# Cross-attention summaries in a decoder layer: one matmul per head on a quarter of TensorE's columns instead of one per group of four heads

## The chip, the cores and the metric

The kernel runs on one core of a Trainium2 chip. The metric is the device time of one execution in microseconds (us). The kernel before took 1000.46 us in the median of three runs (999.9 to 1000.54).

The core has five engines with their own instruction streams: TensorE (PE in the profile; its weight loads are listed apart as PEld), VectorE (DVE), ScalarE (ACT), GpSimd (POOL) and SyncE (SP), which here starts most DMAs. They wait for one another by semaphores. All arrays are fp32.

## What is computed

The reference is a decoder layer over 8 sequences of 112 tokens with 512 features: causal self-attention, cross-attention with linear features, and a mixture of eight experts, each followed by a residual and a layernorm. The change lies in the cross-attention, which has no softmax. Per batch it sums over the 375 context positions once and then applies the sums to the tokens:

```python
x = layernorm(x + attn(x))
q = feature_map((x @ Wq.T) by heads)          # 16 heads of 32; where(x > 0, x + 1, exp(x))
k, v = split(ctx @ Wkv.T);  k = feature_map(k by heads)
kv_summary = einsum('bhsd,bhse->bhde', k, v)  # per head 32 x 32
k_sum = k.sum(axis=-2)                        # per head 32
z = 1.0 / (einsum('bhld,bhd->bhl', q, k_sum)[..., None] + EPS)
attn = einsum('bhld,bhde->bhle', q, kv_summary) * z
x = layernorm(x + (attn * sigmoid(x @ Wg.T + bg)) @ Wo.T)
x = layernorm(x + experts(x))                 # top 2 of 8
```

## The kernel before

Tokens are kept as seven tiles of 128. Weights stream into nine slabs of 1 MB each, which self-attention, cross-attention and experts use in turn. PSUM has four banks for projections (tag `mm`) and four for everything else (`aux`). From the cross-attention on, the order of each engine's instructions is that of the program text.

The cross-attention goes batch by batch (`for b in range(B)`). The 375 positions of a batch are cut into NSC = 3 chunks of SC = 125. `project_pair(n)` makes keys and values of two chunks at once, with a scheme of seven matrix products for eight: `product` issues two matmuls of 512 columns into one of four banks `kvps_..a` to `kvps_..d`, ScalarE and VectorE combine them (`L779` to `L797`), and `mapped` applies the feature map to the keys (`L770` to `L772`). Keys land in `kf` (125 positions x 3 chunks x 512), values in `values`, with an extra column of ones for each group of heads, so that one matmul gives the summary and the key sum. There are two buffers of each; batch b uses buffer b % 2.

`summarize(b)` is the part that changes. It takes the heads in C = 4 groups of four: 128 key features against 128 value columns and the column of ones, summed over the three chunks. Only the four diagonal 32 x 32 blocks of the 128 x 128 result are wanted, so VectorE multiplies by a block-diagonal mask `bdmask`, once for the key sum, spread over the columns (`bdks`, `L820`), and once for the summary (`bdkv`, `L823`). Two groups share a PSUM bank `sumps`, so this comes in two halves.

`attend(b)` multiplies the query features by `bdks` and `bdkv` (`dps` and `nps`, eight matmuls in all of 112 columns, `L833`), and VectorE divides and applies the gate (`L842` to `L845`). `close(b - 1)` then projects one tile of tokens with Wo (`xops`, `L237`), adds, normalizes and routes it: `x2T_ps` (four transposes), `lps` (128 x 8 scores), `cps` (`L540`, `L541`), a long row of short VectorE operations, and later `sTps` (a product with the identity that turns 128 x 8 scores, `L588`) and `dbps`. These chains are advanced by `tick()` between the parts of the loop:

```python
next(work, None)          # first part of project_pair: kvps a and b
tick()
sums = summarize(b)
tick()
if next(work, 0) is None:
    tick()
attend(b, *sums, qf, gate)
```

So in TensorE's order a batch is: two products of the next pair, the summary, two more products (3.4 us in batches 0 to 5), `dps` and `nps`, the rest of the pair. In the last batch nothing is left to project, and the first steps of the experts run in its place.

Of the kernel before, what the change touches and what calls it, by code (L numbers as in the profile page):

```python
# [10 lines left out]
F32 = mybir.dt.float32  # L11
# [8 lines left out]
P = 128  # L20
# [4 lines left out]
C = D // P  # L25
NH, DH = 16, 128
G = 4
SC, NSC = 125, 3
XH = 32
# [16 lines left out]
def decoder_layer(ctx: ExitStack, tc: tile.TileContext, t_in: dict, out: bass.AP):  # L46
    nc = tc.nc
# [12 lines left out]
    def bank(name: str, tag: str = "mm"):  # L60
        return psum.tile([P, 512], F32, tag=tag, name=name)
# [21 lines left out]
    bdmask = const.tile([P, P], F32, name="bdmask")  # L83
# [166 lines left out]
    with tc.tile_pool(name="att", bufs=2) as att:  # L250
# [201 lines left out]
        for h in range(NH + 1):  # L452
            g = h // G
# [231 lines left out]
    with tc.tile_pool(name="cross", bufs=2) as cr:  # L685
# [12 lines left out]
        keys_of = [cr.tile([SC, NSC, 512], F32, name=f"kf{i}", bufs=1) for i in range(2)]  # L698

        values = [  # L700
            cr.tile([SC, NSC, C, P + 1], F32, name=f"values{i}", bufs=1) for i in range(2)
        ]
        for v in values:
            nc.gpsimd.memset(v[:, :, :, P:], 1.0)

        def load_context(b: int):
            cT = cr.tile([P, C, SC * NSC], F32, tag="cT", name=f"cT_{b}")
# [6 lines left out]
        pairs = []  # L714
# [17 lines left out]
        def blocks_of(n: int):  # L732
            one, two = (contexts[b][:, :, sc * SC : (sc + 1) * SC] for b, sc in pairs[n])
            return one[:, low], two[:, low], one[:, high], two[:, high]

        def prepare_pair(n: int):
            if n < len(pairs):
                b11, b12, b21, b22 = blocks_of(n)
                t = room["sums"][n % 2]
                nc.gpsimd.tensor_sub(t[:, 0], b12, b11)  # L740
                nc.gpsimd.tensor_sub(t[:, 1], b22, t[:, 0])
                nc.gpsimd.tensor_sub(t[:, 2], b22, b12)
                nc.gpsimd.tensor_sub(t[:, 3], b21, t[:, 1])

        def project_pair(n: int):

            b11, _, b21, b22 = blocks_of(n)
            t, (e1, e2) = room["sums"][n % 2], room["ends"]
            k1, k2 = (keys_of[b % 2][:, sc, :] for b, sc in pairs[n])
            v1, v2 = (values[b % 2][:, sc, :, :P] for b, sc in pairs[n])  # L750

            def grouped(x):
                return x.rearrange("p (g e) -> p g e", g=C)

            def product(ps, x, w, start: bool):

                for c in range(C // 2):
                    nc.tensor.matmul(
                        ps,
                        x[:, c, :],  # L760
                        w[:, c, :],
                        start=start and c == 0,
                        stop=c == C // 2 - 1,
                        skip_group_check=not start,
                    )

            def mapped(k, name: str):

                tmp = cr.tile([SC, 512], F32, tag="tmp", name=f"{name}_{n}")
                nc.vector.tensor_scalar_min(tmp, k, 0.0)  # L770
                nc.scalar.activation(tmp, tmp, AF.Exp)
                nc.vector.scalar_tensor_tensor(k, k, 0.0, tmp, ALU.max, ALU.add)  # L772


            order = "ab" if n % 2 else "ba"
            got = {i: bank(f"kvps_{n}{i}")[:SC, :] for i in order + "cd"}
            pa, pb, pc, pd = (got[i] for i in "abcd")
            product(pa, b11, wk[:, low], True)
            nc.scalar.copy(e1, pa)  # L779
            product(pb, b21, wk[:, high], True)  # L780
            nc.vector.tensor_add(k1, e1, pb)
            if n != 1:
                prepare_pair(n + 1)
            yield
            product(pa, t[:, 1], wkvs[1], False)
            nc.scalar.copy(e2, pa)
            product(pc, t[:, 0], wkvs[0], True)
            nc.vector.tensor_add(k2, e2, pc)
            mapped(k1, "one")
            yield  # L790
            product(pa, t[:, 2], wkvs[2], False)
            nc.scalar.copy(e1, pa)
            nc.vector.tensor_add(v2, grouped(e1), grouped(pc))
            product(pd, b22, wkvs[3], True)
            nc.vector.tensor_add(k2, k2, pd)
            product(pa, t[:, 3], wv[:, high], False)
            nc.scalar.copy(v1, grouped(pa))  # L797
            mapped(k2, "two")

        def summarize(b: int):  # L800

            kf, vs = keys_of[b % 2], values[b % 2]
            bdkv = cr.tile([P, C, P], F32, tag="bdkv", name=f"bdkv_{b}")
            bdks = cr.tile([P, C, P], F32, tag="bdks", name=f"bdks_{b}")
            mask = bdmask.unsqueeze(1).broadcast_to([P, 2, P])
            for i in range(2):
                ps = bank(f"sumps_{b}_{i}", "aux")
                sums = ps[:, : 2 * (P + 1)].rearrange("p (g e) -> p g e", g=2)
                for j in range(2):
                    g = 2 * i + j  # L810
                    for sc in range(NSC):
                        nc.tensor.matmul(  # L812
                            sums[:, j, :],
                            kf[:, sc, g * P : (g + 1) * P],
                            vs[:, sc, g, :],
                            start=(sc == 0),
                            stop=(sc == NSC - 1),
                        )
                pair = slice(2 * i, 2 * i + 2)
                nc.vector.tensor_mul(  # L820
                    bdks[:, pair, :], mask, sums[:, :, P:].broadcast_to([P, 2, P])
                )
                nc.vector.tensor_mul(bdkv[:, pair, :], mask, sums[:, :, :P])  # L823
            return bdkv, bdks

        def attend(b: int, bdkv, bdks, qf, gate):
# [26 lines left out]
        for n in range(2):  # L853
            for _ in project_pair(n):
                pass
# [8 lines left out]
        for n, w in (("xq", wxq), ("xg", wxg)):  # L864
            for g in range(C):
                for half in range(2):
                    cols = slice(half * HALF, (half + 1) * HALF)
                    ps = bank(f"{n}ps_{g}_{half}")
# [137 lines left out]
        for b in range(B):  # L1006
            if b + 1 < B:

                ns = (3 * b // 2 + 2,) if b % 2 == 0 else (3 * (b + 1) // 2, 3 * (b + 1) // 2 + 1)
                work = itertools.chain.from_iterable(  # L1010
                    itertools.chain(project_pair(n), (None,)) for n in ns
                )
            else:
                work = iter(())
                steps = [start(0, side, "bT")]
                ahead_w.append(fetch_weights(1))
                third = fetch_in_parts(2)
                ahead_w.append(next(third))
            next(work, None)
# [9 lines that stand above are left out]
            if 0 < b < B - 1:  # L1029
                chains.append(close(b - 1))  # L1030
                tick()
            for _ in work:
                tick()
            if b + 3 < B:
                load_context(b + 3)


    with tc.tile_pool(name="moe", bufs=2, reuse_waits="tile") as moe:
# [8 lines left out]
        sums = keep.tile([P, C, T], F32, tag="big", name="sums", bufs=2)  # L1047
        sums = sums.rearrange("p c n -> p (c n)")
# [260 lines left out]
```

## Time and profile before

| | |
|---|---|
| median of three runs | 1000.46 us |
| the profiled execution | 998.96 us |
| its span, first to last instruction | 997.4 us |
| TensorE's granted clock, mean | 0.993 of full speed |
| cross-attention's batches in that span | about 525 to 745 us |
| in 525 to 745: TensorE, VectorE, ScalarE busy | 212.0, 138.0, 60.6 us of 220 |
| summary matmuls (`sumps`), instructions and busy time | 192, 23.4 us |
| idle time of TensorE before `sumps` | 1.8 us, once, for `kf` of batch 1 |
| idle time of VectorE until `sumps` is done | 12.8 us in 16 waits |
| share of the DMA engines busy, 525 to 745 | 0.24; 0.90 in 720 to 760 |

How to read the lines in the prediction: a timeline line gives the start in us from the span's first instruction, the time until the last of the merged instructions ends, the engine, the line of the kernel, the operation, output and inputs, their shapes (weights, then moving operand for a matmul), the count, and in brackets the idle time before and what ended it. Matmuls overlap: one of 129 columns is listed with 0.275 us although the next starts 0.112 us later; the pitch of a row is therefore (time of the row - duration of the last) / (count - 1). A tile query lists each kind of instruction that writes or reads a tile with the shortest, middle and longest duration in ns. A line of the chain of waits gives start, length and what held the end up at that time.

### The profile page before, as it was taken

The numbers are of one execution on the slowest core, as the hardware profiler recorded it, in microseconds if no ns is written. First come the engines' busy times: TensorE is split into PE (matmuls) and PEld (weight loads), VectorE is DVE, ScalarE is ACT, GpSimd is POOL, SyncE is SP. The second block draws the span as 40 slices with busy tenths as digits, with TensorE's granted clock in tenths as the row PEclk, the third lists the DMA queues.
The fourth block names the chain that finished last, engine by engine and source line by source line (L and its number), as shares of the span: only waits on it lengthen the run. The fifth ranks groups of instructions, "written<-read, shape, count | busy, mean of one in ns | idle before, by whom it ended". The sixth has DMA issues, their size and how long they took to land.

```text
span 997.4 us, 9419 instructions
## 1 busy us (share of the span) xinstructions
PE 963.8 (97%) x3271; PEld 505.1 (51%) x3271; DVE 462.5 (46%) x1036; ACT 244.7 (25%) x430; POOL 185.2 (19%) x235
## 2 busy tenths in 40 slices
PE   7998999999999999999999999999899999999994
PEld 3455544566446555654555455555454444444442
DVE  1356511154213542574414566567775533334384
ACT  1132311133103311322222222333124211121132
POOL 3133200033001414020002222211101212111132
PEclk9999999999999999999999999999999999999998
DMA  9990004111010001131001010110489997692333
GB/s 337 367 342 26 1 1 168 43 42 44 0 46 39 1 1 43 43 104 31 1 0 31 9 50 36 53 63 32 151 346 370 328 391 218 202 344 46 95 86 82
DMA packets 33839, 114.99 MB, mean 115 GB/s; under 512 B 3845, under 2 KB 8005, under 8 KB 26240
## 3 DMA queue, kind: packets, MB, share of 16 engines
q1 hardware_dynamic: 26784, 98.28, 26.9%
q0 software_dynamic: 6336, 15.75, 6.6%
q8 instruction: 26, 0.43, 0.2%
q10 hardware_dynamic: 672, 0.36, 0.1%
q14 instruction: 21, 0.17, 0.1%
HBM read 115.83 MB, written 29.01 MB: 145 GB/s over the span
## 4 chain that ended last, share of the span: by engine, by line
PE 86%; DVE 7%; issue 3%; ACT 1%; POOL 1%; DMA 1%; SPq 0%; POOLq 0%; DVEq 0%; ACTq 0%
PE gups L1054 13%; PE ops L237 10%; PE yps L1080 6%; PE vps L327 6%; PE zps L435 3%; PE xqps L870 2%; PE xgps L870 2%; PE sumps L812 2%; PE sps L387 2%; PE xops L237 2%; DVE z L843 1%; PE pps L427 1%; PE aT_ps L975 1%; PE bT_ps L975 1%; DVE p L412 1%
## 5 line engine op out<-in xcount | busy, mean ns | idle before, releaser
L1054 PE MATMUL gups<-slab,bT 128*128 128x512 f32 x336 | 151.5, 593 | 2.0 <-ACT bT L979 2.0
L1054 PEld LDWEIGHTS gups<-slab,bT 128*128 128x128 f32 x336 | 61.9, 190 | 71.4 <-issue 68.4
L237 PE MATMUL ops<-slab,zT 128*128 128x512 f32 x224 | 97.9, 592 | 0.0
L1062 DVE TENSOR_TENSOR gu<-gups,biases 128x512 f32<-128x512 f32 x42 | 29.0, 691 | 114.8 <-PE gups L1054 114.8
L1080 PE MATMUL yps<-slab,aT 128*128 128x512 f32 x168 | 75.9, 595 | 2.3 <-ACT aT L979 2.3
L237 PEld LDWEIGHTS ops<-slab,zT 128*128 128x128 f32 x224 | 42.0, 190 | 50.3 <-issue 49.5
L275 POOL TENSOR_TENSOR ws<-slab 128x256 f32<-128x256 f32 x16 | 11.8, 739 | 282.0 <-PE qk_5c L291 83.0
L327 PE MATMUL vps<-slab,x0T 128*112 128x512 f32 x128 | 58.6, 612 | 1.0 <-DVE x0T L187 0.8
L1094 POOL DMA_INDIRECT total<-y,nums x19 | 30.4, 1602 | 134.6 <-ACT y L1091 61.2
L1080 PEld LDWEIGHTS yps<-slab,aT 128*128 128x128 f32 x168 | 31.2, 190 | 40.6 <-issue 37.1
L244 DVE TENSOR_TENSOR xn<-xn,ops 128x512 f32<-128x512 f32 x28 | 19.2, 685 | 55.3 <-PE ops L237 55.2
L435 PEld LDWEIGHTS zps<-pT,v 112*128 112x128 f32 x256 | 33.5, 192 | 12.3 <-issue 11.2
L327 PEld LDWEIGHTS vps<-slab,x0T 128*112 128x112 f32 x128 | 22.8, 183 | 31.3 <-issue 29.7
L442 DVE COPY zT<-zps 128x448 f32<-128x448 f32 x32 | 20.0, 624 | 39.8 <-PE zps L435 39.8
L411 DVE TENSOR_REDUCE nm<-p 112x4 f32<-112x448 f32 x32 | 19.7, 616 | 30.9 <-POOL p L401 30.9
L435 PE MATMUL zps<-pT,v 112*128 112x112 f32 x256 | 33.4, 273 | 0.0
L1091 ACT COPY y<-yps 128x512 f32<-128x512 f32 x20 | 11.7, 584 | 87.8 <-issue 79.8
L237 PE MATMUL xops<-slab,gate 128*128 128x512 f32 x56 | 27.3, 632 | 3.8 <-DVE gate L845 2.6
L1066 ACT ACTIVATE sg<-gu 128x512 f32<-128x512 f32 x21 | 13.2, 630 | 71.2 <-DVE gu L1064 53.6
L565 POOL DMA_INDIRECT store<-xn,rows x14 | 13.9, 992 | 81.3 <-DVE count L627 52.5
L395 ACT ACTIVATE p<-sps 112x448 f32<-112x448 f32 x32 | 17.4, 544 | 45.6 <-PE sps L387 45.6
L387 PE MATMUL sps<-k,q 128*112 128x112 f32 x256 | 28.0, 262 | 0.0
(799 smaller groups left out, 1649.4 us busy)
## 6 DMA issues: line engine op xcount, KB each, us to landing
slab<-in_wg_dram SPq DMA_DIRECT2D x21, 1024.0 KB
slab<-in_wu_dram SPq DMA_DIRECT2D x21, 1024.0 KB
slab<-in_wd_dram SPq DMA_DIRECT2D x21, 1024.0 KB
store<-slab SPq DMA_DIRECT2D x8, 1806.0 KB
biases<-gubs SPq DMA_DIRECT2D x21, 512.0 KB
cT<-in_ctxT_dram SPq DMA_DIRECT2D x8, 750.0 KB
xblk<-store POOLq DMA_DIRECT2D x21, 258.0 KB, 7.4
slab<-in_wq_dram SPq DMA_DIRECT2D x4, 1024.0 KB
```

The source lines that it names most:

```text
L237: nc.tensor.matmul(ps, aT[:, c, t * P : (t + 1) * P], w[:, c, :], start=(c == 0), stop=(c == C - 1),)
L327: nc.tensor.matmul(ps[:S, :], xT[:, c, b * S : (b + 1) * S], w[:, c, :], start=(c == 0), stop=(c == C - 1),)
L387: nc.tensor.matmul(ps[:S, i * S : (i + 1) * S], qk["q"][:, rows], qk["k"][:, rows], start=True, stop=True,)
L435: nc.tensor.matmul(zps[:, i * S : (i + 1) * S], v[:, half * 4 + i, hl * DH : (hl + 1) * DH], pT[:, i * S : (i + 1) * S], start=True, stop= ...
L442: nc.vector.tensor_copy(zT[:, hl, half * HALF : (half + 1) * HALF], zps[:, :HALF])
L812: nc.tensor.matmul(sums[:, j, :], kf[:, sc, g * P : (g + 1) * P], vs[:, sc, g, :], start=(sc == 0), stop=(sc == NSC - 1),)
L870: nc.tensor.matmul(ps[:, :HALF], w[:, c, g * P : (g + 1) * P], xT[:, c, cols], start=(c == 0), stop=(c == C - 1),)
L975: nc.tensor.transpose(ps[:, c * P : (c + 1) * P], src[:, c * P : (c + 1) * P], ident)
L1054: nc.tensor.matmul(ps, st["bT"][:, c, :], st["w"][k][:, c, :], start=(c == 0), stop=(c == C - 1),)
L1062: nc.vector.tensor_add(a, ps, st["bias"][:, k * I : (k + 1) * I])
L1080: nc.tensor.matmul(ps, st["aT"][:, c, :], st["wd"][:, c, :], start=(c == 0), stop=(c == C - 1 and s < STEPS - 1),)
L1094: put = nc.gpsimd.indirect_dma_start(out=total, out_offset=bass.IndirectOffsetOnAxis(ap=st["num"], axis=0), in_=y, in_offset=None, compute ...
```

## The change

The summary is made head by head. `values` gets a column of ones for each of the NH = 16 heads (XH = 32 columns and one) instead of each group. For each of the four groups and three chunks there are four matmuls, one per head j of the group: 32 key features as weights, 33 moving columns, and the output on PSUM partitions 32j to 32j + 31, which places the head's weights on TensorE's columns 32j to 32j + 31 (a tile of 128 rows x 32 columns). The off-diagonal blocks are not computed. The results of all four groups stand side by side in one PSUM bank, 4 x 33 columns. VectorE then fills `bdks` and `bdkv` with one operation each of 128 x 512 in place of two of 128 x 256, multiplying by the same mask; for `bdkv` the 32 columns of a head are read four times. The rest of the diff adapts the writers of `values` to 16 pieces of 32 columns and the memset of the ones from 4 to 16 columns per chunk.

```diff
         values = [
-            cr.tile([SC, NSC, C, P + 1], F32, name=f"values{i}", bufs=1) for i in range(2)
+            cr.tile([SC, NSC, NH, XH + 1], F32, name=f"values{i}", bufs=1) for i in range(2)
         ]
         for v in values:
-            nc.gpsimd.memset(v[:, :, :, P:], 1.0)
+            nc.gpsimd.memset(v[:, :, :, XH:], 1.0)
...
-            v1, v2 = (values[b % 2][:, sc, :, :P] for b, sc in pairs[n])
+            v1, v2 = (values[b % 2][:, sc, :, :XH] for b, sc in pairs[n])
 
             def grouped(x):
-                return x.rearrange("p (g e) -> p g e", g=C)
+                return x.rearrange("p (h e) -> p h e", h=NH)
...
-            mask = bdmask.unsqueeze(1).broadcast_to([P, 2, P])
-            for i in range(2):
-                ps = bank(f"sumps_{b}_{i}", "aux")
-                sums = ps[:, : 2 * (P + 1)].rearrange("p (g e) -> p g e", g=2)
-                for j in range(2):
-                    g = 2 * i + j
-                    for sc in range(NSC):
+            ps = bank(f"sumps_{b}", "aux")
+            sums = ps[:, : C * (XH + 1)].rearrange("p (g e) -> p g e", g=C)
+            for g in range(C):
+                for sc in range(NSC):
+
+                    for j in range(C):
+                        h = g * C + j
                         nc.tensor.matmul(
-                            sums[:, j, :],
-                            kf[:, sc, g * P : (g + 1) * P],
-                            vs[:, sc, g, :],
+                            sums[j * XH : (j + 1) * XH, g, :],
+                            kf[:, sc, h * XH : (h + 1) * XH],
+                            vs[:, sc, h, :],
                             start=(sc == 0),
                             stop=(sc == NSC - 1),
                         )
-                pair = slice(2 * i, 2 * i + 2)
-                nc.vector.tensor_mul(
-                    bdks[:, pair, :], mask, sums[:, :, P:].broadcast_to([P, 2, P])
-                )
-                nc.vector.tensor_mul(bdkv[:, pair, :], mask, sums[:, :, :P])
+            nc.vector.tensor_mul(
+                bdks,
+                bdmask.unsqueeze(1).broadcast_to([P, C, P]),
+                sums[:, :, XH:].broadcast_to([P, C, P]),
+            )
+            nc.vector.tensor_mul(
+                bdkv.rearrange("p g (j e) -> p g j e", j=C),
+                bdmask.rearrange("p (j e) -> p j e", j=C)
+                .unsqueeze(1)
+                .broadcast_to([P, C, C, XH]),
+                sums[:, :, :XH].unsqueeze(2).broadcast_to([P, C, C, XH]),
+            )
             return bdkv, bdks
```

## The prediction

> **What bounds the kernel now.** I read the page's busy shares first, then its chain of waits, then the tile query for `sumps` (the matmuls that the change rewrites), then the timeline around the first summary, and last the chain of waits of the stage in which the late summaries stand.
>
> ```profile
> span 997.4 us, 9419 instructions
> PE 963.8 (97%) x3271; PEld 505.1 (51%) x3271; DVE 462.5 (46%) x1036; ACT 244.7 (25%) x430; POOL 185.2 (19%) x235
> PE 86%; DVE 7%; issue 3%; ACT 1%; POOL 1%; DMA 1%; SPq 0%; POOLq 0%; DVEq 0%; ACTq 0%
> ...
> L812 PEld LDWEIGHTS sumps<-values,kf x192: 186/192/193, 531.2 to 732.6; 125*128 125x128 f32 x192
> L812 PE MATMUL sumps<-values,kf x192: 272/275/378, 531.6 to 732.8; 125*128 125x129 f32 x192
> L820 DVE TENSOR_TENSOR bdks<-bdmask,sumps x16: 420/422/422, 533.1 to 733.1; 128x256 f32<-128x256 f32 x16
> L823 DVE TENSOR_TENSOR bdkv<-bdmask,sumps x16: 412/414/415, 533.5 to 733.4; 128x256 f32<-128x256 f32 x16
> ```
>
> PE is on 86% of the chain, so time taken from or given to TensorE in the middle of its stream is time of the kernel, unless another engine is the bound at that place. The code calls 8 x 4 x 3 = 96 summary matmuls and the trace has 192: each fp32 matmul is two pairs of weight load and matmul, both on the same place of the array.
>
> ```profile
> 531.59 2.85 PE L812 MATMUL sumps<-values,kf 125*128 125x129 f32 x24
> 533.13 0.42 DVE L820 TENSOR_TENSOR bdks<-bdmask,sumps 128x256 f32<-128x256 f32 x1 [0.58 <-PE sumps L812]
> 534.47 0.42 DVE L820 TENSOR_TENSOR bdks<-bdmask,sumps 128x256 f32<-128x256 f32 x1 [0.59 <-PE sumps L812]
> 534.81 0.41 DVE L823 TENSOR_TENSOR bdkv<-bdmask,sumps 128x256 f32<-128x256 f32 x1
> 537.71 1.04 PE L833 MATMUL dps<-qf,bdks 128*128 128x112 f32 x8
> ```
>
> A summary is 24 pairs: (2.85 - 0.275) / 23 = 0.112 us from one to the next, 2.68 us in all, 21.5 us for the eight batches. After it `dps`, the first reader of `bdks`, starts 2.5 us after `bdkv` is done: here VectorE's tail is covered. Not so in the stage of batches 6 and 7:
>
> ```profile
> 704.06 2.89 PE sumps L812 x24
> 706.98 0.42 DVE bdks L820
> 707.40 0.33 DVE bdkv L823
> ...
> 713.59 0.68 DVE kf L788
> ...
> 720.88 0.64 DVE gate L845
> 721.56 5.25 PE xops L237 x8
> ...
> 730.35 2.68 PE sumps L812 x24
> 733.03 0.81 PE lps L515 x8
> ```
>
> From 706.98 to 721.56 the chain runs on VectorE without a break: what it does later after a summary, TensorE waits for.
>
> **What the Trainium skill says.** "TensorEngine Tiling (Array Packing)", Key Properties: the 128 x 32 tiles can load weights and multiply in parallel, and a change of the tiling mode, not of the tile, drains TensorE. The drain is in this trace: `sTps` (8 columns of weights, in the same 128 x 32 mode) stands directly before batch 3's summary.
>
> ```profile
> 603.75 1.88 PE L758 MATMUL kvps_6b<-slab,cT 128*125 128x512 f32 x4
> 605.55 0.10 PEld L588 LDWEIGHTS sTps<-ident,sco 128*8 128x8 f32 x2 [0.76 <-DVE xn L222]
> 605.55 0.38 PE L588 MATMUL sTps<-ident,sco 128*8 128x128 f32 x2
> 605.87 2.75 PEld L812 LDWEIGHTS sumps<-values,kf 125*128 125x128 f32 x24 [0.22 <-issue]
> 605.87 2.94 PE L812 MATMUL sumps<-values,kf 125*128 125x129 f32 x24
> ```
>
> The weight load that normally starts with the matmul before it starts at 605.55, 0.09 us later than the 0.43 us pitch of `kvps_6b` asks (605.03 + 0.43 = 605.46); leaving the mode, the second `sTps` matmul starts at 605.66, the next weights at 605.87, and the summary takes 2.94 instead of 2.85: 0.20 us lost against a pitch of 0.11. "TensorE: Matmul & The Clock Gate", Back-to-back issue gap, says that matmuls of 1 to 64 columns all take about 60 cycles, 25 ns; this trace agrees: the two 8-column `cps` matmuls, x2 in 0.29 us with 0.256 for the later one, start 0.03 apart. The same page, Part 3, has tiles 4 ns apart and speed-ups of 2.38 for three column tiles, but at 512 columns, and matmuls strictly in order. No run here shows matmuls on different column tiles.
>
> **The change part by part.**
>
> *Matmuls.* 24 pairs of 128 weight columns and 129 moving columns become 96 pairs of 32 and 33, per batch. The pitch of pairs bound by moving columns is 0.43 us at 512 and 0.376 at 448 (12 `xgps` in 4.67 us, one 0.539), so 0.84 ns a column and 3 ns: 33 columns take 30 ns. The load of 128 columns has a pitch of 0.112, the two of 8 columns in `sTps` lie 0.10 - 0.087 = about 0.01 apart: 32 columns take about 28 to 32 ns. Thus one pair after the other takes 30.5 ns: 96 x 0.0305 = 2.93 us, against 2.68: +0.25 us a batch, +2.0 us for eight. Work is not saved: four times the instructions at a quarter of the length, unless the quarters overlap. Bounds: 8 ns a pair if four quarters run fully in parallel (0.8 us), 57 ns (30 + 27) if a load is not hidden behind a matmul. I take 30.5. The reason is the two pairs of each fp32 matmul: the second load wants the same quarter, whose spare weights come free only when the first matmul starts, and the loads of the next quarter stand behind it. A hidden load I take as shown: within `sTps`, in this mode, the second load begins 0.01 us after the first and the matmuls keep their 0.11.
>
> *Mode switches.* Entry costs 0.09 plus the exposed 32-column load, 0.12; exit 0.20. By neighbours in TensorE's order: batches 0 and 2 pay both (+0.64); batch 1 only the exit (+0.20), for its entry lies in the 1.8 us wait for `kf`; batches 3, 4 and 5 pay nothing, since the `sTps` before them has the mode already and the exit only moves behind the summary; batch 6 gains 0.20 (its exit moves beside the VectorE stretch); batch 7 pays the entry, 0.12, and its exit hides behind the longer `bdkv`. Sum +0.76 us.
>
> *VectorE.* Two pairs of 256-column operations become one of 512. The 512-column operations of batch 6 (`L772`, then `L596`, then the next) follow each other at 0.61 in the timeline, the 256-column ones here at 0.34; so I take 0.61 each. Per batch 1.34 becomes 1.22, but none of it can start before the last summary matmul, so `bdkv` ends 1.22 instead of 0.67 after it: +0.55. `dps` in batches 0 to 5 is at least 3.4 us away (eight matmuls at 0.43), and the routing operations queued behind (batches 2 and 4) end 1.3 us before their next partner. In batch 6 VectorE is the bound, and in batch 7 `lps`'s reader stands behind `bdkv`: +0.55 each, +1.1 us. If the doubly broadcast `bdkv` took twice as long there, it would be +1.2 more; below nothing is excluded by the start.
>
> *Edits at nothing.* The `values` writes by VectorE and ScalarE keep 512 elements (0.68 and 0.585 us) in runs of 32; the same elements decide. The two memsets grow from 125x12 (0.119 us) to 125x48, at 436.9 on a POOL that waits there. One bank less is taken per summary, which can only shorten bank waits. No DMA is added or moved; those that wait on routing shift with it.
>
> *Sum.* +2.0 + 0.76 + 1.1 = +3.9 us. The profiled execution took 998.96 us (span 997.4 and 1.6 around it), which gives 1002.8; the runs' median is 1000.46, 1.5 more than the profiled one, so a median of 1004.3.
>
> **The rivals.** *Overlapping quarters (faster).* If the next quarter's load is taken past the waiting second load, two quarters are at work at once: about 16 ns a pair, 1.54 us a batch, -1.14 x 8 = -9.1, +1.9 for switches and VectorE: -7.2, 993.2. For full overlap 8 to 10 ns, -12, 988. For it: the skill's parallel tiles, the diff's inner loop over quarters, and a queue that issues three `sTps` instructions within 0.01 us. Against: the loads in this trace never start before the preceding matmul has, and the floor of 25 to 30 ns already bites at 33 columns. The point of decision is 28 ns a pair, where 96 pairs equal 2.68.
>
> *Exposed loads (much slower).* If changing the quarter keeps the next load from going under the running matmul, 57 ns a pair: 5.5 us, +2.8 x 8 + 1.9 = +24, 1024.8. Against: the hidden load inside `sTps`; but that never changes its quarter.
>
> *The change is neutral.* Pairs at 28 ns and a covered VectorE tail leave the switches alone: +0.8, within what counts as no change.
>
> **How the numbers follow.** One after another 0.50 (1002.3 to 1005.5, pairs from 28 to 32 ns), overlap 0.36, exposed loads or worse 0.14. A measurement of this kernel can tell 0.2%, 2 us, from none. Faster 0.36; of the first case 0.06 falls within 2 us; slower 0.44 + 0.14 = 0.58. The range takes in the first case and the two-quarter overlap with room, 990 to 1009, and leaves out full overlap and exposed loads. The slower cases alone: 1002 to 1009, the long tail apart.
>
> **What would show it.** Right: `sumps` x768 with about 30 ns from one to the next and some 2.9 to 3.2 us a batch; the gap of 0.2 us after the summary, no longer between `sTps` and it; `bdks` and `bdkv` x8 at about 0.69 us each; `xops` of batch 6 later by half a microsecond against its summary. Wrong: `sumps` of a batch within 2 us (overlap), or over 4 us (exposed loads, or a price per instruction that no row of before shows).

## The result and the profile after

The changed kernel took 987.4 us in the median of four runs (985.63 to 990.45), against 1000.5 us of the kernel before on the same chip. The ratio is 0.9875 with a 95% interval of 0.9849 to 0.9901: 10 to 15 us less. A second set on another chip gave 0.9893 (0.9876 to 0.9910). The forecast was 1004.3 us, slower; the measured time lies below its range.

The page of the changed kernel, its span, TensorE's busy time and the chain of waits by engine:

```profile
span 984.0 us, 10556 instructions
PE 949.3 (96%) x3847; PEld 490.5 (50%) x3847; DVE 461.0 (47%) x1020; ACT 244.7 (25%) x430; POOL 185.2 (19%) x235
...
PE 84%; DVE 9%; issue 3%; ACT 2%; POOL 1%; DMA 1%; POOLq 0%; DVEq 0%; SPq 0%; ACTq 0%
```

TensorE is the bound as before, with 576 pairs of weight load and matmul more and 14.5 us less busy time; VectorE's part of the chain grew from 7% to 9%. The tile query for `sumps` (shortest, middle, longest duration in ns):

```profile
L812 PEld LDWEIGHTS sumps<-values,kf x768: 105/109/114, 531.9 to 717.1; 125*32 125x32 f32 x192
L812 PE MATMUL sumps<-values,kf x768: 190/197/218, 531.9 to 717.1; 125*32 125x33 f32 x192
L819 DVE TENSOR_TENSOR bdks<-bdmask,sumps x8: 686/689/689, 533.0 to 717.3; 128x512 f32<-128x512 f32 x8
L824 DVE TENSOR_TENSOR bdkv<-bdmask,sumps x8: 679/680/682, 533.6 to 717.9; 128x512 f32<-128x512 f32 x8
```

The instructions are those that were expected, and so are VectorE's durations: 0.689 and 0.680 us, the doubly broadcast read included. What was not expected shows in the timeline of the first summary:

```profile
531.37 0.59 PE L758 MATMUL kvps_2b<-slab,cT 128*125 128x512 f32 x1
...
531.89 0.92 PEld L812 LDWEIGHTS sumps<-values,kf 125*32 125x32 f32 x96 [0.76 <-issue]
531.89 1.03 PE L812 MATMUL sumps<-values,kf 125*32 125x33 f32 x96
...
532.86 1.98 PE L758 MATMUL kvps_2a<-slab,biases 128*125 128x512 f32 x4
532.96 0.69 DVE L819 TENSOR_TENSOR bdks<-bdmask,sumps 128x512 f32<-128x512 f32 x1 [0.21 <-PE sumps L812]
533.57 0.68 DVE L824 TENSOR_TENSOR bdkv<-bdmask,sumps 128x512 f32<-128x512 f32 x1
```

96 pairs in 1.03 us: (1.03 - 0.197) / 95 = 8.8 ns from one to the next, where one after the other, at the price of the prediction, they would need 30.5 ns. Between three and four are at work at any time. The summary, 2.68 us of TensorE's stream before, is 0.84 now.

### The profile page after: what moved, and what is told of

It reads as the page before. It is cut to its first block, busy times and chain, and to the rows that moved or that the text cites. A ratio compares the mean times of both kernels' runs of the same rounds, so it can differ in the third digit from the quotient of the medians.

```text
span 984.0 us, 10556 instructions
## 1 busy us (share of the span) xinstructions
PE 949.3 (96%) x3847; PEld 490.5 (50%) x3847; DVE 461.0 (47%) x1020; ACT 244.7 (25%) x430; POOL 185.2 (19%) x235
## 4 chain that ended last, share of the span: by engine, by line
PE 84%; DVE 9%; issue 3%; ACT 2%; POOL 1%; DMA 1%; POOLq 0%; DVEq 0%; SPq 0%; ACTq 0%
PE gups L1061 14%; PE ops L237 10%; PE yps L1087 7%; PE vps L327 6%; PE zps L435 3%; PE xqps L877 2%; PE xgps L877 2%; PE sps L387 2%; DVE z L850 2%; PE xops L237 1%; PE pps L427 1%; PE aT_ps L982 1%; PE bT_ps L982 1%; DVE p L412 1%; PE sumps L812 1%
## 5 line engine op out<-in xcount | busy, mean ns | idle before, releaser
L275 POOL TENSOR_TENSOR ws<-slab 128x256 f32<-128x256 f32 x16 | 11.8, 738 | 281.7 <-PE qk_5c L291 83.0
L327 PEld LDWEIGHTS vps<-slab,x0T 128*112 128x112 f32 x128 | 22.9, 184 | 31.4 <-issue 29.7
```

What stands on the lines that cost most here:

```text
L327: nc.tensor.matmul(ps[:S, :], xT[:, c, b * S : (b + 1) * S], w[:, c, :], start=(c == 0), stop=(c == C - 1),)
```

## The experiments

All of them change only `summarize` (one also the layout of `values`, one also the buffers of `bdkv`); the time of the kernel before on the same chip stands beside each.

### One quarter after the other

```diff
-            for g in range(C):
-                for sc in range(NSC):
-                    for j in range(C):
+            for j in range(C):
+                for g in range(C):
+                    for sc in range(NSC):
```

> The same 96 pairs a batch, reordered so that the 24 pairs of one column quarter stand in a row, then the next quarter. Theory (the quarters overlap, each takes a new pair every 30 ns or so): 30 ns from pair to pair, 2.8 to 3.0 us a summary, about 1002 to 1005 us in all, as the prediction had it for the changed kernel. Rival (a short pair is cheap wherever it goes, no overlap needed): 8.5 ns a pair and 1.0 us a summary as in the changed kernel, about 987 us.

Measured: 1003.96 us against 999.09, ratio 1.0056 (1.0036 to 1.0075). First summary in the timeline:

```profile
532.02 2.93 PE L812 MATMUL sumps<-values,kf 125*32 125x33 f32 x96
534.88 1.98 PE L758 MATMUL kvps_2a<-slab,biases 128*125 128x512 f32 x4
```

(2.93 - 0.196) / 95 = 28.8 ns a pair as a mean of the whole row. Inside the 24 pairs of one quarter the starts in the trace lie 31.7 ns apart; the mean is lower because the end of one quarter's run and the start of the next overlap, three times in a batch. The same instructions, the same work, in an order that leaves three quarters idle most of the time: the gain is gone, and with the mode switches and VectorE's longer tail the kernel is slower than before the change. This is very nearly the kernel that the prediction described (30.5 ns, +3.9 us; here 31.7 ns, +3.6 to +7.5). The summaries account for the difference from the changed kernel: 985.63 + 8 x (2.93 - 1.03), and 1.7 for one more stretch at half clock (last section), give 1002.5 us, and the profiled execution took 1002.34. The rival, that short pairs are cheap wherever they go, falls.

So does another: in this order six pairs in a row add into the same place of PSUM, and that might hold them up, not the quarter. But every seventh pair begins another sum, in other columns of PSUM, and starts 31 ns after the one before it, against 32 within a sum.

### Two quarters in turn

```diff
-            for g in range(C):
-                for sc in range(NSC):
-                    for j in range(C):
+            for pair in ((0, 1), (2, 3)):
+                for g, sc in itertools.product(range(C), range(NSC)):
+                    for j in pair:
```

> The same 96 pairs, alternating between two quarters only (first 0 and 1, then 2 and 3). Overlap theory: half of 30 ns, so 15 to 16 ns a pair and 1.5 to 1.7 us a summary, about 992 to 994 us. Rival (short pairs cheap anyway): 8.5 ns and 1.0 us, about 987 us.

Measured: 988.82 us against 999.09, ratio 0.9899 (0.9865 to 0.9933).

```profile
531.64 1.62 PE L812 MATMUL sumps<-values,kf 125*32 125x33 f32 x96
```

(1.62 - 0.195) / 95 = 15.0 ns as a mean. Where the row runs steadily, the starts lie 15.8 ns apart; they lie 31.7 apart on one quarter, and 8.3 in the changed kernel, whose row starts more slowly. So the price of a pair is that of its quarter, some 32 ns, divided by the quarters in turn; at four a little of it, 8.3 - 31.7 / 4 = 0.4 ns, is lost. The total was 3 to 5 us lower than expected. The trace says why: its summary has the pitch that was expected, but TensorE had full clock throughout its work, while the two profiled executions of the changed kernel had one and two stretches at half clock (last section). From the first of them, 985.63 - 1.7 + 8 x (1.62 - 1.03) = 988.6 us; the profiled execution here took 988.41.

### Six pairs in a row on one quarter

```diff
-                for sc in range(NSC):
-                    for j in range(C):
+                for j in range(C):
+                    for sc in range(NSC):
```

> The same 96 pairs in the order group, head, chunk: six pairs in a row on one quarter, then six on the next. It tells how far TensorE's queue looks past a blocked pair. If it looks past one blocked load only: most of the six run one after the other, 25 to 30 ns a pair, 2.4 to 2.9 us a summary, 999 to 1004 us. If it looks over some 16 pairs: two or three quarters at work, 10 to 15 ns, 1.1 to 1.6 us a summary, 988 to 993 us.

Measured: 991.32 us against 999.09, ratio 0.9943 (0.9923 to 0.9964).

```profile
532.87 1.78 PE L812 MATMUL sumps<-values,kf 125*32 125x33 f32 x96
```

(1.78 - 0.196) / 95 = 16.7 ns: about two quarters at work at a time, a little slower than the 10 to 15 ns expected of a queue that looks far. The seven runs fall into two groups, four of 990.9 to 991.3 us and three of 994.8 to 995.0 with a lower mean clock (0.992 against 0.995).

How far the queue looks can be counted in the trace. Starts on one quarter lie 29 ns or more apart, so a pair that starts within 20 ns of the one before it must be on another quarter. In each of the eight batches the first such pair comes when three of the six pairs have started and three are waiting. With 24 pairs in a row (`one_quarter`) it comes after 21, again with three waiting. So the queue passed three waiting pairs and not a fourth. The natural nesting of the loops (a head's three chunks together) would have given away about two fifths of what the summary gained: 1.78 us, against 2.85 before and 1.03 in the changed kernel.

### Two heads a matmul on two column halves

```diff
-                    for j in range(C):
-                        h = g * C + j
+                    for j in range(2):
+                        h = g * 2 + j
                         nc.tensor.matmul(
-                            sums[j * XH : (j + 1) * XH, g, :],
-                            kf[:, sc, h * XH : (h + 1) * XH],
+                            sums[j * 2 * XH : (j + 1) * 2 * XH, g, :],
+                            kf[:, sc, h * 2 * XH : (h + 1) * 2 * XH],
```

with a column of ones per two heads in `values`; the masks clear the blocks off the diagonal.

> Two heads a matmul: 64 key features by 65 columns on two column halves, 48 pairs a batch, the mask clears the two blocks off the diagonal. Overlap theory: a half takes a pair every 57 ns, two at once 28 to 29 ns, 48 pairs 1.4 us; about 5 us slower than the changed kernel, some 991 to 993 us, and the 0.2 us gap between sTps and the summary comes back if 128 x 64 is another mode than 128 x 32. Without overlap: 57 ns a pair, 2.7 us, some 1001 to 1003 us.

Measured: 991.78 us against 999.09, ratio 0.9924 (0.9897 to 0.9951). The timeline at the summary that follows `sTps`:

```profile
604.13 0.39 PE L588 MATMUL sTps<-ident,sco 128*8 128x128 f32 x2
...
604.45 1.48 PEld L811 LDWEIGHTS sumps<-values,kf 125*64 125x64 f32 x48 [0.22 <-issue]
604.45 1.62 PE L811 MATMUL sumps<-values,kf 125*64 125x65 f32 x48
```

(1.62 - 0.222) / 47 = 29.7 ns a pair of 65 columns, where one after the other they would take some 57 by the prediction's price: the halves overlap as the quarters do. The next weight load waits from 604.25 (the second `sTps` matmul) to 604.45, so 128 x 64 is a mode of its own, and this version pays switches that the quarters share with `sTps`.

### VectorE's masks in two halves

```diff
-            ps = bank(f"sumps_{b}", "aux")
-            sums = ps[:, : C * (XH + 1)].rearrange("p (g e) -> p g e", g=C)
-            for g in range(C):
+            for i in range(2):
+                ps = bank(f"sumps_{b}_{i}", "aux")
+                sums = ps[:, : 2 * (XH + 1)].rearrange("p (g e) -> p g e", g=2)
...
+                pair = slice(2 * i, 2 * i + 2)
+                nc.vector.tensor_mul(
+                    bdks[:, pair, :],
```

> The changed kernel with the results of two groups each in a bank of their own, and VectorE's masking in two halves of 128 x 256 as before the change, so that the first half can start when half of the summary is done. Theory (VectorE's longer tail of 0.55 us is on the path in batches 6 and 7 only): the tail after the summary shrinks from 1.22 to about 0.9 us, the two stretches together give 0.6 to 0.8 us, nothing in batches 0 to 5, so 0.7 us faster than the changed kernel. Rival (the tail is covered, or the prediction's 0.55 was elsewhere): no difference in the lead at the xops of batch 6.

The changed kernel went along in the same rounds:

> The changed kernel once more, on the chip and in the rounds of the next two, to compare them with. As before: 984 to 990 us, where the executions differ by the number of 3.4 us stretches in which TensorE is granted half its clock (1.7 us each); a summary of 1.03 us.

Measured: 986.54 us against 999.11, ratio 0.9871 (0.9851 to 0.9891); the changed kernel in the same rounds 987.84, 0.9893 (0.9876 to 0.9910). The intervals overlap, so the times do not tell the two apart. VectorE in batch 6, whose last summary matmul ends at 695.57:

```profile
695.18 0.42 DVE L820 TENSOR_TENSOR bdks<-bdmask,sumps 128x256 f32<-128x256 f32 x1
695.52 0.41 DVE L825 TENSOR_TENSOR bdkv<-bdmask,sumps 128x256 f32<-128x256 f32 x1
695.85 0.41 DVE L820 TENSOR_TENSOR bdks<-bdmask,sumps 128x256 f32<-128x256 f32 x1
696.18 0.41 DVE L825 TENSOR_TENSOR bdkv<-bdmask,sumps 128x256 f32<-128x256 f32 x1
```

The tail ends 1.02 us after the summary instead of 1.32, and `xops` of batch 6 starts 14.85 us after it instead of 15.15: the 0.30 us arrive in full. In batch 7 the gate operation comes 6.68 us after the summary instead of 6.88. In batches 0 to 5 the distance from the summary to `dps` is unchanged to 0.01 us. The theory holds in the trace; the effect, half a microsecond where 0.6 to 0.8 was expected, is below what the times can show.

### ScalarE writes the blocks of bdkv

```diff
-            nc.vector.tensor_mul(
-                bdkv.rearrange("p g (j e) -> p g j e", j=C),
...
-            )
+            for j in range(C):
+                rows = slice(j * XH, (j + 1) * XH)
+                nc.scalar.copy(bdkv[rows, :, rows], sums[rows, :, :XH])
```

with two buffers for `bdkv` that GpSimd zeroes once.

> The changed kernel with bdkv written by ScalarE: four copies of the 32 x 4 x 32 diagonal blocks from PSUM into two buffers zeroed once by GpSimd, beside VectorE's bdks. Theory (the VectorE tail is on the path in batches 6 and 7): VectorE is free 0.61 us after the summary instead of 1.22, ScalarE about 1 us after it: up to 1.2 us faster than the changed kernel, less what the row of short routing operations loses by waiting for ScalarE. Rival (TensorE or ScalarE takes the place): no gain, or a loss where ScalarE's copies delay the activation in the routing.

Measured: 986.93 us against 999.11, ratio 0.9877 (0.9858 to 0.9896): not to be told from the changed kernel. The timeline of batch 6, whose summary ends at 694.32:

```profile
694.36 0.69 DVE L822 TENSOR_TENSOR bdks<-bdmask,sumps 128x512 f32<-128x512 f32 x1 [0.40 <-PE sumps L815]
...
695.08 1.06 ACT L829 COPY bdkv<-sumps 32x128 f32<-32x128 f32 x4 [1.31 <-DVE bdks L822]
...
696.17 0.20 ACT L558 ACTIVATE ex<-d 128x1 f32<-128x1 f32 x1
```

ScalarE did not run beside VectorE: its copies wait for `bdks` and end 1.82 us after the summary, and the routing's `ex`, which VectorE needs, stands behind them. VectorE is free at 0.73 instead of 1.32, but `xops` comes 14.85 us after the summary, no earlier than with the halves. Whether copies that really start with `bdks` would bring more stays open.

## Why the prediction was wrong

The forecast named the right quantity and the right three prices around it, and took the wrong value for it. By its steps:

**The pitch of the matmuls: wrong, and with it the sign.** The step that failed is "I take 30.5" and its reason, that "the loads of the next quarter stand behind" the second load of the same fp32 matmul. They do not. Behind `sTps`, which uses one quarter, the changed kernel's timeline has:

```profile
601.17 0.10 PEld L588 LDWEIGHTS sTps<-ident,sco 128*8 128x8 f32 x2 [0.76 <-DVE xn L222]
601.18 0.28 PE L588 MATMUL sTps<-ident,sco 128*8 128x128 f32 x1
601.19 1.10 PEld L812 LDWEIGHTS sumps<-values,kf 125*32 125x32 f32 x96
601.19 0.26 PE L812 MATMUL sumps<-values,kf 125*32 125x33 f32 x6
...
601.29 0.27 PE L588 MATMUL sTps<-ident,sco 128*8 128x128 f32 x1
```

The two `sTps` matmuls stand first in the program. The second has to wait 0.11 us for its quarter, and meanwhile six summary matmuls start. Both loads and matmuls of a free quarter pass a pair that waits, though not without limit: from 601.26, when the six have started, to 601.40 no further pair starts. With that, the term became 8 x (0.84 - 2.68) = -14.7 us instead of +2.0.

**The floor of 25 to 30 ns per matmul** is not the engine's: over four quarters pairs start every 8.8 ns. The two 8-column `cps` matmuls from which it was read both use the whole array, and could not show whose floor it is. Whether a quarter has a floor of its own is not shown here: its 31.7 ns are little more than the streaming of 33 columns (28 ns at 0.84), and on a half a pair of 65 columns takes about 58. The 3 ns that the prediction adds to 0.84 ns a column don't follow from the two rows that it names, but its price for one pair after another, 30.5, was nearly right. The prediction had both ends, 8 and 30.5, with an argument for each, and gave the lower end 0.36 together with the two-quarter case; its range stopped at the latter. What would have helped is in its own evidence: the speed-up of 2.38 for three column tiles, which it quotes from the Trainium skill ("TensorE: Matmul & The Clock Gate", Part 3, Measured speedup vs the span model), was measured, while the argument against it was an inference on the queue's order from rows that never change the quarter.

**The overlap rival** gave -12 us, 988, for full overlap at 8 to 10 ns, and 987.4 was measured. Its sum with the measured pitch is -14.7 + 0.76 + about 0.9 = -13.0. The traces give a little less. The profiled executions before and after differ by 998.96 - 985.63 = 13.3 us, but the earlier one has two stretches of 3.41 us at half TensorE clock inside its busy time and the later has one; at 1.7 us each, 11.6 us are left. The second profile of the changed kernel has two as well: 997.4 - 985.6 = 11.8 us of span. Before the cross-attention the two executions of the changed kernel were already 0.22 and 0.86 us behind the kernel before, which the change did not cause. With that the change is worth some 11.8 to 12.6 us; where the rest of the 13.0 went stays open.

**The mode switches** came as priced. Entry: 531.89 against 531.37 + 0.43 = 531.80, 0.09 us, and the load after it. Exit: the last summary matmul starts at 531.89 + 1.03 - 0.20 = 532.72, the next load at 532.85, and the `kvps_2a` row is 0.10 longer than its usual 1.88: 0.2 us. Behind `sTps` there is no gap any more; it lies after the summary.

**VectorE's tail** came nearly as priced. It ends 1.32 us after the summary instead of 0.79, and the chain of waits of the late batches shows it on the path:

```profile
693.06 0.86 PE sumps L812 x74
693.95 0.69 DVE bdks L819
694.63 0.60 DVE bdkv L824
...
701.09 0.68 DVE kf L788
...
708.38 0.64 DVE gate L852
709.06 3.72 PE xops L237 x8
...
716.32 0.98 PE sumps L812 x90
...
719.66 0.23 DVE both L532
```

From the end of the summary (693.91) to `xops` it is 15.15 us, before 14.62: +0.54 for the predicted 0.55. In batch 7, from 717.28 to `both`, it is 2.38. The kernel before, whose summary ends there at 733.03, has

```profile
735.01 0.23 DVE both L532
```

thus 1.98: +0.40, less than the 0.55. In batch 0 `dps` starts 3.46 us after the summary, before 3.27, the difference being the exit of the mode: the tail is covered there.

**The edits at nothing** cost nothing that the trace shows, and exposed loads did not occur.

## What to carry to other kernels

Matmuls with at most 32 weight columns should go to the four column quarters in turn, innermost in the loop: a pair with 33 moving columns costs its quarter about 32 ns and the engine a quarter of that, but only if the next pairs in the program go to other quarters: here no more than three waiting pairs were passed. Put such groups next to each other, since entering and leaving the tile mode costs 0.3 us, and look at who reads the result: an operation that now waits for the whole group may stand on the path in one stage though it is covered in the others. When a forecast hangs on one price with two bounds of opposite sign, and only an inference on order stands against the better one, the range has to hold both.

## What the runs showed of the hardware

- Matmuls overtake one another: six on other quarters started before an earlier one whose quarter was busy (601.19 to 601.26 against 601.29), so order holds for a quarter at most. The look ahead is short: in `one_quarter` and `runs_of_three` the first pair of another quarter started when three pairs were still waiting before it, in every batch, and not while four were. The Trainium skill's "TensorE: Matmul & The Clock Gate", Part 3, What overlaps and what doesn't, on which the prediction leaned, has matmuls in strict order; the trace decides otherwise.
- A short pair occupies its quarter, not the engine: at 33 moving columns 31.7 ns a pair on one quarter, 15.8 on two in turn, 8.3 on four, where the row runs steadily.
- TensorE was granted half its clock for single stretches of 3.41 us, none to three of them in a profiled execution apart from its end. Each costs 1.7 us of busy TensorE, and they explain part of the spread of 985.6 to 990.5 us between runs of the changed kernel (mean clock 0.995 to 0.987). Of the 16 in the nine traces, 13 come directly after 3.41 us in which TensorE was busy for less than half of the time: 0.86 us of them before the one of the changed kernel at 735.30. Three, all between 609 and 616 us, come in a stream without a gap. Not every such lull is followed by one: the second profile of the changed kernel has 1.38 us busy in 88.15 to 91.57 and keeps its clock. What sets them off was not tried.
